# Layer 0 attention: transposes without padding, keys of the second batch earlier, and scores, all values, scores, other work in each group of heads

## The chip, the cores and the metric

The kernel runs on one core of a Trainium2 chip. A core has five engines with a queue each: TensorE (PE: matrix products, and transposes as products with an identity; its weight loads are listed apart as PEld), VectorE (DVE), ScalarE (ACT), GpSimd (POOL) and SyncE (SP, which here issues DMAs). Each works through its own instructions in order and waits on semaphores for the others. The metric is the device time of one execution in microseconds (us); lower is better.

## The reference

Four layers, each a cross attention and a feed-forward part with residuals and layer norms, on x of 4 batches x 256 tokens x 256, with a context of 512 tokens x 128 per batch. The change is in layer 0's attention:

```python
q = (x @ Wq + bq).reshape(b, s1, H, HD)          # H = 16 heads of HD = 16
k, v = from y_main @ Wk, y_main @ Wv             # 496 context tokens
k_dca, v_dca = from y_dca @ Wkv_dca              # the last 16 context tokens
q = _ln(q, qn_w, qn_b); k = _ln(k, kn_w, kn_b); k_dca = _ln(k_dca, kn_dca_w, kn_dca_b)
ctx = softmax(q k^T / 4) v + softmax(q k_dca^T / 4) v_dca      # per head
return ctx @ Wo + bo
```

The norms are per head, over its 16 values. The two softmaxes, over 496 and 16 tokens, are separate.

## The kernel before, in words

`bounded_path` (L837) computes everything in one launch; `general_path` runs only if a bound on the scores is exceeded. Layer 0 stands in a block with a manual schedule: on PE, ACT, DVE and POOL the order of the program is the order of the queue.

**Setup of batch 0** (L1482 to L1527): context transposes, layer norm, projections, `Scale` for queries and keys, `transposed`. `brow` shares the tile tag of kT, `rep` that of qT0; `norm_columns` (L1252) spreads the norm's weights from `rep` over the partitions as columns `cols`.

**Per batch.** `project_q` (L1170), `project_k` (L1186) and `project_v` (L1199) are products into PSUM; DVE adds the bias into `qk`, ACT copies values. `Scale` (L1212) normalises all heads: `square` on POOL (ACT in the setup), `sum` on DVE, `power` on ACT (Ln, then Exp), `product` on DVE, which writes the normalised heads into the single tile `pad`. There every head has 32 columns, of which the upper 16 are zero. `transposed` (L1306) turns pad's six chunks (two of queries, four of keys), with four transposes of 128x128 per chunk, one per group of heads, into one PSUM bank per chunk; the bank is evicted into qT or kT with the norm's weight and bias, by ACT for even chunks, by DVE for odd ones (L1330, L1328). In kT and qT a head then has a strip of 32 partitions, and 16 of them are used.

**Per group of four heads** (hg, four groups per batch). `scores` (L1334) for half the keys (kp 0 or 1): eight products (two chunks of keys x four heads), each head in its own strip of rows of the array; four PSUM banks, one per head; four exponentials on ACT (L1345) into pT. `values` (L1347): the four heads in four strips of columns, over two chunks of keys, plus four products for the 16 extra tokens (L1360). A column block of ones in the values gives the softmax sums. `quotient` (L1368): on DVE transpose, reciprocal, transpose, product (L1374 to L1382); on POOL the sums into oT. `output0` (L1389) projects a finished batch.

**Order.** One group runs behind: the values are those of the group before (`before`). The loop calls, per half i = 2 hg + kp: `scores`, `ahead(b, i)`, half the values, after the second half `quotient`, then `between(b, i)`. `ahead` and `between` (L1534, L1543) hold the other work, mostly the preparation of batch n = b + 1: i = 0 layer norm and context transposes, 1 queries, 2 keys and square, 3 values and sum, 4 power, 5 product and the statistics of batch n + 1, 6 the first three chunks of `transposed`, 7 the other three; `output0` of the batch before at 6 and 7. In the last batch the same places hold the first pieces of the feed-forward part (`Norm`, `Arrows`), the mask (`mf`, `pmk`, L1586 to L1591) and `output0`.

**PSUM.** Eight banks: two with tag "o" (the values' results), and a ring of six that scores, projections and transposes take in turn (L851). Whoever takes a bank waits until the one that had it six allocations before is evicted.

## Time and profile before

| what | value |
|---|---|
| median of 4 runs | 1416.97 us (1415.1 to 1422.18) |
| the profiled execution, its own time | 1416.62 us |
| its span | 1414.9 us |
| mean granted TensorE clock | 0.995 |
| first score matmul of layer 0 | 24.2 us |
| last value matmul ends, feed-forward products begin | 152.3 us |

Busy time of the engines in layer 0's stretches, in us, with the granted TensorE clock:

| stretch, us | holds | PE | DVE | ACT | POOL | clock |
|---|---|---|---|---|---|---|
| 24 to 56 | groups of batch 0 | 29.59 | 18.36 | 19.94 | 10.33 | 0.89 |
| 56 to 92.3 | batch 1 | 34.97 | 23.56 | 21.55 | 8.95 | 0.95 |
| 92.3 to 123.9 | batch 2 | 31.60 | 18.93 | 21.43 | 8.92 | 1.00 |
| 123.9 to 152.3 | batch 3 | 28.40 | 21.68 | 19.84 | 8.18 | 1.00 |
| 152.3 to 230 | feed-forward of layer 0 | 77.03 | 57.15 | 38.45 | 25.63 | 1.00 |

How to read it: in the timeline a line has the start, the busy time, the engine, the line of the code, the operation, out<-in, shapes and the number of instructions, and in brackets how long the engine was idle before and what ended that. "issue" means that it waited for nothing that the profile shows. Every fp32 product is two instructions, a transpose one. Matmul ends are modelled, so a busy PE is not PE at its peak; gaps between weight loads tell more.

### The profile page before, as it was taken

What the parts mean: (1) busy time and instruction counts of PE and PEld (TensorE: products, weight loads), DVE (VectorE), ACT (ScalarE), POOL (GpSimd) and SP (SyncE); (2) the same over time, 40 slices, a digit from 0 to 9 for tenths busy, and PEclk for the clock granted to TensorE, in tenths of its full rate; (3) what the DMA queues carried; (4) which work ended last, traced back from release to release, by engine and by line L of the source; (5) the groups of instructions that cost most, each with busy time, mean ns of one, the idle gap of its engine ahead of it and who ended that gap; (6) DMA issues with size and microseconds to landing.
All of it is one profiled execution on the core that took longest, in us unless ns stands there. A gap on an engine that the chain in (4) does not pass through costs nothing.

```text
span 1414.9 us, 20097 instructions
## 1 busy us (share of the span) xinstructions
PE 1395.2 (99%) x7339; PEld 921.7 (65%) x7339; DVE 893.9 (63%) x2004; ACT 586.3 (41%) x1156; POOL 677.4 (48%) x809
## 2 busy tenths in 40 slices
PE   9999999999999999999999999999999999999997
PEld 7566667566566666887555666666975656666666
DVE  5667874675765657654576656558655667566675
ACT  5567464433434332256443334333554343333331
POOL 3223322576554455132576654656214864445560
PEclk9999999999999999999999999999999999999999
DMA  5000120310000000273110000000421000000000
GB/s 164 2 1 2 60 75 16 77 37 1 8 0 8 1 8 1 65 219 95 38 53 8 16 1 8 0 0 16 145 71 60 5 1 1 1 1 0 1 1 33
DMA packets 48871, 46.01 MB, mean 33 GB/s; under 512 B 8185, under 2 KB 44762, under 8 KB 48764
## 3 DMA queue, kind: packets, MB, share of 16 engines
q1 hardware_dynamic: 45308, 36.90, 8.7%
q0 software_dynamic: 2352, 6.43, 1.6%
q8 instruction: 60, 0.98, 0.3%
q10 hardware_dynamic: 1104, 1.31, 0.3%
q14 instruction: 47, 0.39, 0.1%
HBM read 38.20 MB, written 6.42 MB: 32 GB/s over the span
## 4 chain that ended last, share of the span: by engine, by line
PE 91%; DVE 4%; POOL 2%; issue 1%; ACT 1%; DVEq 0%; POOLq 0%
PE ps L1856 22%; PE po L1864 22%; PE paq L1826 6%; PE pao L1826 5%; PE pbq L1826 4%; PE pbo L1826 4%; PE ps L1341 2%; PE paf L1425 2%; PE pgu L2379 2%; PE po L1351 2%; PE pyf L1475 2%; PE psh L2201 1%; PE py L1946 1%; PE pm L986 1%; PE pn L1002 1%
## 5 line engine op out<-in xcount | busy, mean ns | idle before, releaser
L1875 POOL TENSOR_TENSOR half<-pT 128x1024 f32<-128x1024 f32 x93 | 218.2, 2347 | 289.1 <-ACT pT L1859 217.3
L1856 PE MATMUL ps<-qT,cT 128*128 128x512 f32 x768 | 345.7, 593 | 0.0
L1864 PE MATMUL po<-pT,c_sb 128*128 128x512 f32 x768 | 345.3, 592 | 0.0
L1859 ACT ACTIVATE pT<-ps,mbias 128x512 f32<-128x512 f32 x384 | 263.8, 687 | 155.8 <-PE ps L1856 142.8
L1864 PEld LDWEIGHTS po<-pT,c_sb 128*128 128x128 f32 x768 | 146.0, 190 | 183.1 <-issue 183.1
L1856 PEld LDWEIGHTS ps<-qT,cT 128*128 128x128 f32 x768 | 139.0, 191 | 138.3 <-issue 136.7
L1868 ACT COPY oT<-po 128x512 f32<-128x512 f32 x96 | 56.3, 586 | 265.0 <-PE po L1864 265.0
L1911 POOL TENSOR_TENSOR oT<-oT,wide 128x512 f32<-128x512 f32 x90 | 114.3, 1290 | 17.3 <-DVE wide L1910 17.3
L1836 DVE TENSOR_TENSOR qT<-qT,paq 128x128 f32<-128x128 f32 x90 | 25.4, 282 | 95.1 <-ACT qT L1835 95.1
L1345 ACT ACTIVATE pT<-ps 128x512 f32<-128x512 f32 x128 | 65.9, 604 | 36.5 <-PE ps L1341 36.3
L1836 DVE TENSOR_TENSOR w<-w,pao 128x128 f32<-128x128 f32 x21 | 6.0, 285 | 106.6 <-ACT w L1835 106.6
L1883 DVE TENSOR_TENSOR half<-half 128x512 f32<-128x512 f32 x96 | 71.3, 742 | 2.7 <-POOL half L1873 2.5
L1885 DVE STREAM_TRANSPOSE turned<-half 128x512 f32<-128x512 f32 x96 | 68.3, 711 | 6.3
L1826 PE MATMUL paq<-xnT_a,m_sb 128*128 128x128 f32 x360 | 71.4, 280 | 0.0
L1826 PE MATMUL paq<-xx,m_x 128*128 128x128 f32 x360 | 69.6, 275 | 0.0
L1826 PEld LDWEIGHTS paq<-xnT_a,m_sb 128*128 128x128 f32 x360 | 57.3, 192 | 17.2 <-issue 8.7
L1889 DVE TENSOR_REDUCE sums<-turned 128x16 f32<-128x512 f32 x96 | 65.8, 686 | 3.3
L1826 PE MATMUL pao<-n_x,ox 128*128 128x128 f32 x336 | 65.2, 276 | 0.3 <-POOL ox L1752 0.3
L1835 ACT COPY qT<-paq 128x128 f32<-128x128 f32 x90 | 23.9, 265 | 94.1 <-PE paq L1826 94.1
L1910 DVE STREAM_TRANSPOSE wide<-rz 128x512 f32<-128x512 f32 x96 | 62.2, 685 | 0.1
L1839 DVE TENSOR_TENSOR qT<-qT,pbq 128x384 f32<-128x384 f32 x90 | 49.8, 554 | 9.4
L1826 PEld LDWEIGHTS paq<-xx,m_x 128*128 128x128 f32 x360 | 54.7, 192 | 0.0
(456 smaller groups left out, 2567.0 us busy)
## 6 DMA issues: line engine op xcount, KB each, us to landing
wq<-in_L_wqT SPq DMA_DIRECT2D x11, 512.0 KB, 5.3
wo<-in_L_wo SPq DMA_DIRECT2D x11, 512.0 KB, 7.0
yd<-yr SPq DMA_DIRECT2D x20, 128.0 KB, 4.7
w<-in_F_w SPq DMA_DIRECT2D x4, 512.0 KB, 3.3
xd<-xn_f SPq DMA_DIRECT2D x7, 256.0 KB, 2.1
wk<-in_L_wkT SPq DMA_DIRECT2D x11, 128.0 KB, 4.0
wv<-in_L_wvT SPq DMA_DIRECT2D x11, 128.0 KB, 5.0
x_sb<-in_x SPq DMA_DIRECT2D x4, 256.0 KB, 3.1
```

The source lines that it names most:

```text
L1345: nc.scalar.activation(pT[kp][:, j], ps[j], AF.Exp)
L1826: nc.tensor.matmul(p[:, at, :], lhsT=lhsT, rhs=rhs, start=(k == 0 and at == 0), stop=(k == len(of) - 1 and i == which[-1]),)
L1856: nc.tensor.matmul(ps, lhsT=cT[:, b, k * P : (k + 1) * P], rhs=qT, start=True, stop=True)
L1859: nc.scalar.activation(pT[:, k, :], ps, AF.Exp, bias=mbias[:, b, k : k + 1])
L1864: nc.tensor.matmul(po, lhsT=c_sb[:, b, k, :], rhs=pT[:, k], start=(k == 0), stop=(k == NK - 1))
L1868: done["head"] = nc.scalar.copy(raw, po).ins
L1875: nc.gpsimd.tensor_tensor(half, pT[:, 0:2], pT[:, 2:4], ALU.add)
L1883: nc.vector.tensor_tensor(part, half[:, 0], half[:, 1], ALU.add)
L1885: nc.vector.transpose(turned.rearrange("p f i -> p (f i)"), part)
L1889: nc.vector.tensor_reduce(sums[b, hp // 4][:, hp % 4, :], turned, AX.X, ALU.add)
L1910: nc.vector.transpose(wide, rzs[b, hp // 4][:, hp % 4, :, None].to_broadcast([P, NB, 32]))
L1911: eng.tensor_tensor(outs[b, hp], outs[b, hp], wide.rearrange("p f i -> p (f i)"), ALU.mult)
```

## The change

1. **Transposes without padding.** `pad` becomes [128, 6 chunks, 2, 128]: 16 heads of 16 columns without gaps, eight heads to a transpose. `transposed` is called for two chunks, with four transposes into one bank. A strip of 32 partitions now holds two heads (o = 0, 1). The keys are evicted as they are (kT uses two of its four planes); the queries are evicted twice, once per o, with columns `cols[:, o]` that are zero for the other head's 16 rows. Scores contract over 32 rows. ACT evicts queries o = 0 and keys 0 to 255, DVE queries o = 1 and keys 256 to 511, with a second small operation for the 16 extra tokens. Heads are numbered (q j o) instead of (q o j), so `wo0`, the biases and `wvo` are rearranged; `rep` has eight rows, filled by two POOL copies and one DVE copy; `brow` has its own tile.
2. **Early keys.** For batch n = 1: keys at i = 0 (before the layer norm's transposes), square at 1, sum at 2, power at 3, product at 4.
3. **Order per group.** Scores of half 0; all values of the group before, and its quotient; in group 3 all of `transposed(b + 1)`; scores of half 1; then `ahead` and `between` of both halves. In the first group of batch 0, which has no values, `between(0, 0)` stays between the two score calls.

```diff
-        brow = w0.tile([1, 2, 2 * D], F32, tag="kT", name="brow")
-        rep = w0.tile([1, 6, 4, 32], F32, tag="qT0", name="rep")
+        brow = l0.tile([1, 2, 2 * D], F32, tag="brow", name="brow")
+        rep = w0.tile([1, 8, 4, 2, HD0], F32, tag="qT0", name="rep")
...
-        pad = l0.tile([P, NQK * H0, 32], F32, tag="pad", name="pad")
-        nc.vector.memset(pad[:, :, HD0:], 0.0)
+        pad = l0.tile([P, NQK, 2, P], F32, tag="pad", name="pad")
...
-                self.dst = pad.rearrange("p (c h) x -> p c h x", h=H0)[:, a:z, :, :HD0]
+                self.dst = pad.rearrange("p c q (h x) -> p c (q h) x", x=HD0)[:, a:z]
...
-            for i in range(6):
+            for i in range(8):
...
-        def transposed(b, chunks):
+        def transposed(b, c0):
...
-            for c in chunks:
-                pt = bank("t", [P, 4, P], f"pT{b}_{c}")
-                for hg in range(4):
-                    r0 = c * H0 + 4 * hg
-                    nc.tensor.transpose(
-                        pt[:, hg, :], pad[:, r0 : r0 + 4, :].rearrange("p h x -> p (h x)"), ident
-                    )
...
+            pt = bank("t", [P, 2, 2, P], f"pT{b}_{c0}")
+            for c in range(2):
+                for q in range(2):
+                    nc.tensor.transpose(pt[:, c, q, :], pad[:, c0 + c, q, :], ident)
+            if c0 < NC:
+                src = pt.rearrange("p c q t -> p q c t")
+                for o in range(2):
+                    dst = qT.rearrange("p (q o) (c t) -> p o q c t", o=2, c=2)[:, o]
+                    if o:
+                        nc.vector.tensor_scalar(dst, src, cols[:, o, 0:1], cols[:, o, 1:2], ALU.mult, ALU.add)
+                    else:
+                        nc.scalar.activation(dst, src, AF.Identity, bias=cols[:, o, 1:2], scale=cols[:, o, 0:1])
+            else:
...
+                if k0:
+                    nc.vector.tensor_scalar(wide, src, cols[:, 2, 0:1], cols[:, 2, 1:2], ALU.mult, ALU.add)
+                    nc.vector.tensor_scalar(
+                        wide[:, :, 1, RD:], src[:, :, 1, RD:], cols[:, 3, 0:1], cols[:, 3, 1:2], ALU.mult, ALU.add
+                    )
                 else:
...
+                    nc.scalar.activation(wide, src, AF.Identity, bias=cols[:, 2, 1:2], scale=cols[:, 2, 0:1])
...
-                    r = slice(32 * j, 32 * j + HD0)
+                    r = slice(32 * j, 32 * j + 32)
                     k0 = (2 * kp + k) * P
                     nc.tensor.matmul(
-                        ps[j][:, k, :], lhsT=kTs[b][r, hg, k0 : k0 + P], rhs=qTs[b][r, hg, :], start=True, stop=True
+                        ps[j][:, k, :], lhsT=kTs[b][r, hg // 2, k0 : k0 + P], rhs=qTs[b][r, hg, :], start=True, stop=True
                     )
...
+        for o in range(2):
+            nc.gpsimd.tensor_copy(rep[:, 2 * o : 2 * o + 2, :, o, :], prm[:, 0, :, None, :].to_broadcast([1, 2, 4, HD0]))
...
             n = b + 1
             if n < B:
-                if i == 5:
+                if i == (4 if n == 1 else 5):
                     scale[n].product()
-                elif i == 7:
-                    transposed(n, range(3, NQK))
...
                 if i == 0:
+                    if n == 1:
+                        for k0 in range(0, NK, 2):
+                            project_k(n, k0)()
                     xnTs[n] = layernorm_T(xns[n], f"a0_{n}")
...
-                elif i == 2:
+                elif i == 2 and n > 1:
                     for k0 in range(0, NK, 2):
                         project_k(n, k0)()
+                elif i == 3 and n > 1:
+                    project_v(n)
+                if i == (1 if n == 1 else 2):
                     scale[n] = Scale(n, 0, NQK)
                     scale[n].square(False)
...
-                for kp in range(2):
-                    scores(b, hg, pT, kp)
-                    ahead(b, 2 * hg + kp)
-                    if before:
-                        if kp == 0:
-                            po = bank("o", [P, 2, S], f"po0_{b}_{hg}")
-                        values(*before, po, (2 * kp, 2 * kp + 1), kp == 1)
-                        if kp == 1:
-                            quotient(*before[:2], po, oTs[before[0]])
-                    between(b, 2 * hg + kp)
+                scores(b, hg, pT, 0)
+                if before:
+                    po = bank("o", [P, 2, S], f"po0_{b}_{hg}")
+                    values(*before, po, range(NK), True)
+                    quotient(*before[:2], po, oTs[before[0]])
+                else:
+                    between(b, 0)
+                if hg == 3 and b + 1 < B:
+                    for at in range(0, NQK, 2):
+                        transposed(b + 1, at)
+                scores(b, hg, pT, 1)
+                for i in (2 * hg, 2 * hg + 1) if before else (1,):
+                    ahead(b, i)
+                    between(b, i)
                 before = (b, hg, pT)
```

## The prediction

> **What bounds the kernel now.** I read the page first, then the chain of waits and the timeline of the first 230 us, then granted clock in half-microsecond stretches. The change touches only layer 0's attention, from its first score matmul at 24.2 us to the last value matmul at 152.3 us.

> ```profile
> span 1414.9 us, 20097 instructions
> ## 1 busy us (share of the span) xinstructions
> PE 1395.2 (99%) x7339; PEld 921.7 (65%) x7339; DVE 893.9 (63%) x2004; ACT 586.3 (41%) x1156; POOL 677.4 (48%) x809
> ```

> TensorE (PE) is the bound, so time saved on it counts until another engine makes it wait. The weight loads (PEld) in the timeline show what a turn costs when there is no other work between score calls (L1341) and value calls (L1351, L1360):

> ```profile
> 109.33 0.74 PEld L1341 LDWEIGHTS ps<-qT,kT 16*128 16x128 f32 x16 [0.33 <-issue]
> 110.41 0.59 PEld L1351 LDWEIGHTS po<-pT,vals 128*32 128x32 f32 x16 [0.33 <-issue]
> 111.41 1.01 PEld L1341 LDWEIGHTS ps<-qT,kT 16*128 16x128 f32 x16 [0.41 <-ACT pT L1345]
> 112.75 0.59 PEld L1351 LDWEIGHTS po<-pT,vals 128*32 128x32 f32 x16 [0.33 <-issue]
> 113.42 0.35 PEld L1360 LDWEIGHTS po<-pT,vals_d 128*32 128x32 f32 x8
> ```

> Each turn from scores to values leaves a gap of 0.33 us, each turn from values to anything 0.41; between L1351 and L1360, both values, there is none. I read the gap as the price of changing the array's shape. The other losses come from VectorE (DVE), as the chain of waits of 79 to 95 us shows:

> ```profile
> 79.05 1.76 DVE pad L1245
> 80.81 0.64 DVE z L1374
> ...
> 82.51 0.69 DVE o L1382
> 83.20 0.34 DVE st_a L918
> ...
> 84.31 0.58 DVE ve_a L920
> 84.90 0.72 DVE qT L1328
> 85.62 0.04 issue
> 85.67 1.13 PE ps L1341 x10
> ```

> Product, quotient, layer-norm statistics, then the eviction of one transposed bank: PE stood still from 84.34 to 85.67 because score bank j=3 is the ring bank that this eviction frees (six banks, taken in turn). The stop has a sequel in the granted clock. Columns: stretch, its length, PE's busy time (instructions), PEclk, DMA share, GB/s:

> ```profile
> 84.50:85.00 0.50, 0.00 (x0) 1.00 0.00 0
> 85.50:86.00 0.50, 0.33 (x6) 1.00 0.00 0
> 86.50:87.00 0.50, 0.50 (x4) 0.77 0.00 0
> 87.00:87.50 0.50, 0.50 (x4) 0.50 0.00 0
> 90.00:90.50 0.50, 0.50 (x16) 0.82 0.00 0
> ```

> From 86.8 to 90.2, 3.4 us, PE ran at half clock: up to 1.7 us lost for a wait of 1.33. The same follows the wait of 1.77 at 49.78 (half clock 52.7 to 56.1), and there is a third such stretch at 28.7.

> **What the change removes from PE.** (1) Transposes: 12 instead of 24 per batch. Twelve loads take 1.29 us (L1316 at 116.26), 0.107 each; 48 fewer are 5.1 us. (2) Turns. Value calls that are followed by something else: 29 before (15 groups of two halves, less the one that runs into the last call), 15 after: 14 x 0.41 = 5.7. Score calls: 32 such ends before, 27 after, since in five places (batch 0 after groups 1, 2, 3; batches 1 and 2 after group 2, counted from 0) nothing stands between two score calls: 5 x 0.33 = 1.7. Returns from full-size matmuls to scores (0.17 at 95.38): 21 to 15, 1.0; three returns from transposes to values at about 0.28 vanish, 0.8. Together 9.2. Sum: -14.3 us.

> **What it costs nothing, or little.** Scores now load 32 rows instead of 16: a 16-row load takes 185 ns, a 128-row one 190, and the matmuls 374 against 379, with four at once; 0 to +0.8 us, I take 0 (32 is nearer 16). The product writes pad densely; 1.76 for 1536 elements stays, as L1382's dense 512 take 0.69, no less per element. Evictions keep 512 elements at 0.79 (ACT) or 0.80 (DVE); ACT has 2 instead of 3 per batch, DVE 2 and a small one (0.33) instead of 4. POOL's two copies into rep (nearest POOL copy 0.3 each) run from 16.1, when POOL has nothing until 24.2, and end before norm_columns reads at 17.07; that has four more instructions at 0.12, 0 to 0.5, hidden since the key transposes wait for pad until 22.14 anyway: 0. The DMAs keep their number.

> **Waits that the new order makes.** Below, t is the start of a score call; its first exponential starts 1.23 later (109.33 to 110.56) and the four take 2.06.

> (a) Scores on scores: the ring has two free banks, the third and fourth come free when the first two exponentials of the call before end (t+1.8, t+2.3). PE wants them from t+0.94 on: 1.0 us. Once each in batches 1 and 2 and between batches 0 and 1: 3.0. In batch 0, `power` is queued on ACT ahead of the next group's exponentials and waits for the DVE sum; walking the queues on from the first scores at 23.7, the sum ends at 38.4, power at 39.05, and the exponentials that could start at 37.2 start then; PE stands at the ring three times, 1.0+1.2+1.3 = 3.5. In batch 3, 0.6. Sum 7.1.

> (b) Batches 1, 2, first group: xnT's copy now stands on ACT behind the second score call's exponentials: ready at 1.23+2.06+0.6 = t+3.9, while PE, after scores 1.07 and two sets of transposes 1.02, wants the query projection at t+2.1. 1.7 each: 3.4. Before, scores and values lay between.

> (c) Batches 1, 2: power stands behind the exponentials of the call at t: 3.29, Ln and Exp 0.6, product 2.63 (78.18 to 80.81): pad is ready at t+6.6; PE, after the next scores (done at t+2.75 with a), a turn of 0.33, all values 1.7 and a turn of 0.41, wants it at t+5.2. 1.4 each: 2.7.

> (d) Before the last score call of a batch: bank j=3 is the query transposes' bank. DVE must first do product, statistics 1.45 (not in batch 2), quotient 2.5, eviction 0.8. In batch 1: 6.6+1.45+2.5+0.8 = t+11.4; PE, after pad at 6.6, transposes 1.3 and three score matmuls, is there at t+8.4: 3.0. Batch 2: 9.9 against 8.4, 1.5. In batch 0 keys and product come one slot earlier; walked on from above, pad is ready at 44.0, the chain ends at 48.75, PE is there at 46.8: 1.9. Sum 6.4. Queued behind: four exponentials, both output projections, the next batch's scores.

> (e) Batch 3: pmk's transpose waits for mf, now behind the quotient on DVE (2.5, then the cast 0.64, PE has 1.1 to do): 2.1. (f) The last value call follows the last scores at once; its second half needs their exponentials (t+3.3; PE is there after 0.74+0.33 and half the values 0.67, at t+1.8, and its loads run on a little ahead): 1.3 to 1.5, I take 1.3.

> Added: 7.1+3.4+2.7+6.4+2.1+1.3 = 23.0. Removed: 1.77 and 1.33 (above), about 1.4 at 43.7 to 45, 1.2 in the start (keys need two evictions, not four), some 1.0 of small ones: 6.7. Waits: 23.0-6.7 = +16.3. Without the clock: -14.3+16.3 = +2.0.

> **Clock.** There are some seven places with waits over 1.3. Half clock costs nothing where PE would have waited anyway, as between (c) and (d), so I take five stretches at 1.5, 7.5, against 3 x 1.7 = 5.1 now: +2.4. Bounds: no more loss than now, 0; eight stretches at 1.7, +8.5. [...]

> Sum +4.4, against the profiled execution's 1416.62 (span 1414.9 plus 1.7 around it, 0.35 below the median of the runs shown): **1421 us**. After the attention PE is busy 77.03 of 77.70 us to 230, so what it gains or loses there is carried on.

> **Rivals.** *Clock gate (slower).* The waits of (b), (c), (d), (e) and (f) each draw a stretch of half clock: eight at 1.7 give +2.0+8.5 = +10.5, 1427. It decides from six to seven stretches on. For it: both waits of that size now did so. Against: a stretch that falls on a wait costs nothing. 0.28. *Turns aren't saved.* If the gaps were the tail of the matmuls and paid anyway, 9.2 come back: +13.6, 1430. Against: no gap at 113.42. 0.05. *Waits half as long (faster).* If exponentials and DVE keep up better than one chain after another, as where the query eviction precedes the quotient, 23.0 becomes 11.5: -14.3+11.5-6.7 = -9.5, 1407. Against: the queues are in program order, and the wait for j=3 is there now. 0.14. *My case*, 0.53.

> A measurement tells 0.5% (7.1 us) from no change. Within: 1409.9 to 1424.05. Range 1408 to 1431: the low end reaches to the faster case, the high one to both slower ones.

> **What would show it.** After: 48 transposes on L1316's successor; values in one run of 40 loads; PE waits of about 3 us for DVE qT before the last scores of batch 1, 1.7 for xnT before the query projections, 2 for mf; the attention ending near 156 instead of 152.3. PEclk in the slices 1 to 4 tells the clock. I am wrong if the j=3 wait is missing, or if PE runs through at full clock.

## The result, and the profile after

| | before | after |
|---|---|---|
| median | 1416.86 us (78 runs, 1413.07 to 1424.75) | 1419.81 us (48 runs, 1418.49 to 1423.09) |
| the profiled execution | 1416.62 us | 1421.25 us |
| first score load to last value load of layer 0's attention, by the timeline | 24.15 to 151.75: 127.6 us | 24.13 to 153.28: 129.15 us |
| stretches of half clock in it (3.4 us each) | 3 | 1 |

The ratio is 1.002, with a 95% interval of 1.0013 to 1.0026: 2.95 us slower, too little to count as a change by the bound of 0.5%, but not nothing. The page of the changed kernel begins:

```profile
span 1419.5 us, 19996 instructions
## 1 busy us (share of the span) xinstructions
PE 1390.4 (98%) x7295; PEld 918.8 (65%) x7295; DVE 889.5 (63%) x1999; ACT 584.1 (41%) x1152; POOL 678.4 (48%) x811
```

PE has less to do (1390.4 us instead of 1395.2) and needs longer: it waits more. The list of PE's waits between 20 and 160 us shows for what (us in total, times, longest):

```profile
PE pT L1319 <- DVE pad L1249: 3.6, 4, 1.2
PE pq L1178 <- ACT xnT_a L941: 3.3, 2, 1.7
PE pmk L1600 <- DVE mf L1596: 1.8, 1, 1.8
PE ps L1347 <- DVE qT L1325: 1.0, 1, 1.0
PE py L1399 <- DVE qT L1325: 1.0, 1, 1.0
PE ps L1347 <- ACT pT L1351: 0.9, 3, 0.3
PE ps L1347 <- ACT kT L1338: 0.4, 1, 0.4
PE ps L1347 <- DVE kT L1334: 0.4, 1, 0.4
```

The list of before in the same stretch:

```profile
PE pT L1316 <- DVE qT L1328: 1.8, 1, 1.8
PE ps L1341 <- DVE qT L1328: 1.3, 1, 1.3
PE pT L1316 <- ACT qT L1330: 0.5, 1, 0.5
PE pxn_a L938 <- DVE xn_a L926: 0.4, 1, 0.4
PE ps L1341 <- ACT pT L1345: 0.2, 1, 0.2
```

It comes to 4.2 us. In the changed kernel pad, xnT, mf and qT are there, as forecast. But PE's list counts modelled ends, and shows only 0.9 us for score calls that wait for exponentials. The weight loads show more. In the timeline of batch 1, group 2:

```profile
73.91 1.45 PEld L1357 LDWEIGHTS po<-pT,vals 128*32 128x32 f32 x32 [0.33 <-issue]
75.45 0.35 PEld L1366 LDWEIGHTS po<-pT,vals_d 128*32 128x32 f32 x8
76.21 1.16 PEld L1347 LDWEIGHTS ps<-qT,kT 32*128 32x128 f32 x20 [0.41 <-ACT pT L1351]
78.08 0.29 PEld L1347 LDWEIGHTS ps<-qT,kT 32*128 32x128 f32 x2 [0.71 <-ACT pT L1351]
78.57 0.72 PEld L1347 LDWEIGHTS ps<-qT,kT 32*128 32x128 f32 x10 [0.20 <-ACT pT L1351]
79.63 1.45 PEld L1357 LDWEIGHTS po<-pT,vals 128*32 128x32 f32 x32 [0.33 <-issue]
```

The values run in one piece, 73.91 to 76.21: 2.30 us. The two score calls behind them stand one on the other and take 3.42 us (76.21 to 79.63); a call with something else behind it takes 1.07 (89.36 to 90.43), two 2.14. The 0.71 and the 0.20 are the ring: the third and the fourth bank come free with the exponentials.

The chain of waits through the last group of batch 1, which answers to the one shown of before:

```profile
81.24 1.76 DVE pad L1249
83.00 0.35 DVE st_a L918
...
84.28 0.63 DVE z L1380
...
85.97 0.69 DVE o L1388
86.66 0.73 DVE qT L1325
87.39 0.04 issue
87.43 1.99 PE py L1399 x8
```

Product, statistics, quotient and eviction are still in a row on DVE. What waits for the eviction at the end is now the output projection (py), not the last score call.

The granted clock (columns as in the windows of before):

```profile
52.50:53.00 0.50, 0.50 (x8) 0.67 0.00 0
53.00:53.50 0.50, 0.50 (x6) 0.50 0.00 0
...
87.00:87.50 0.50, 0.07 (x1) 1.00 0.00 0
90.00:90.50 0.50, 0.50 (x16) 1.00 0.00 0
```

Half clock comes once in the attention, at 52.7; where before had it, at 86.8 to 90.2, the clock is full, though PE stood still just ahead of it (1.0 us for qT, up to 87.43).

**Where the time came from.** From the end of the attention to 560 us every product of the changed kernel starts 1.52 us later than in before's profile. Then, between 590 and 645 us, in layer 1's expert part, whose code is the same, it loses another 3.7 us; from there to the end the shift stays near 5.2. Experiments 8 and 11 come back to these 3.7 us.

### The profile page after: what moved, and what is told of

Read it like the earlier page. It is cut to its first block, busy times and chain, and to the rows that moved or that the text cites. A ratio compares the mean times of both kernels' runs of the same rounds, so it can differ in the third digit from the quotient of the medians.

```text
span 1419.5 us, 19996 instructions
## 1 busy us (share of the span) xinstructions
PE 1390.4 (98%) x7295; PEld 918.8 (65%) x7295; DVE 889.5 (63%) x1999; ACT 584.1 (41%) x1152; POOL 678.4 (48%) x811
## 4 chain that ended last, share of the span: by engine, by line
PE 89%; DVE 4%; POOL 2%; issue 2%; ACT 1%; DMA 1%; DVEq 0%; POOLq 0%; ACTq 0%
PE ps L1870 22%; PE po L1878 22%; PE paq L1840 6%; PE pao L1840 5%; PE pbq L1840 4%; PE pbo L1840 4%; PE ps L1347 2%; PE paf L1431 2%; PE pyf L1481 2%; PE po L1357 2%; PE psh L2215 1%; PE pgu L2393 1%; PE py L1960 1%; PE pm L986 1%; PE pn L1002 1%
## 5 line engine op out<-in xcount | busy, mean ns | idle before, releaser
L1351 ACT ACTIVATE pT<-ps 128x512 f32<-128x512 f32 x128 | 65.8, 605 | 35.3 <-PE ps L1347 35.3
```

The costliest lines, as they stand in the source:

```text
L1351: nc.scalar.activation(pT[kp][:, j], ps[j], AF.Exp)
```

## The experiments

Theory at the start: the order saves turns and gives them back as waits, made by the work that now stands behind the second score call. Rivals: half clock decides; the new transposes cost. "Attention" below is the time from the first score load to the last value load in a run's profile, with its stretches of half clock.

**1. The old order, the rest as changed.**

```diff
-                scores(b, hg, pT, 0)
-                if before:
...
-                    values(*before, po, range(NK), True)
+                for kp in range(2):
+                    scores(b, hg, pT, kp)
+                    ahead(b, 2 * hg + kp)
+                    if before:
...
+                        values(*before, po, (2 * kp, 2 * kp + 1), kp == 1)
...
+                    between(b, 2 * hg + kp)
```

In place 6 stands transposed(n, 0), in place 7 of `ahead` the other two.

> The changed kernel with the order of before: transposes without padding and early keys stay; scores, half the values, scores, the other half and the other work alternate as before, and the transposes stand in the places they had. Theory (the order saves turns but gives them back as waits, the unpadded transposes are a gain by themselves): the 48 transposes fewer give 48 x 0.107 = 5.1 us against before, two evictions fewer in the start about 1, so 1410 to 1412, ratio to before 0.996; 48 transposes in the trace, value loads in halves with a turn of 0.41 us after each, and the wait for the query bank before a batch's last score call still there. Rival 1 (the order is a gain, the new transposes and 32-row scores cost): slower than the changed kernel, 1421 or more. Rival 2 (half clock decides): three stretches of half clock in the attention as in before and a time within 2 us of before.

Measured: 1409.53 us, ratio 0.9939 (0.992 to 0.9959), half a microsecond under the range expected; attention 116.77 us, no half clock in it. The theory holds: the order alone costs 10.3 us against this kernel, and the other two parts gain 7.3. Its timeline shows the same kind of group as above:

```profile
70.61 1.01 PEld L1347 LDWEIGHTS ps<-qT,kT 32*128 32x128 f32 x16 [0.41 <-ACT pT L1351]
71.95 0.59 PEld L1357 LDWEIGHTS po<-pT,vals 128*32 128x32 f32 x16 [0.33 <-issue]
72.63 0.35 PEld L1366 LDWEIGHTS po<-pT,vals_d 128*32 128x32 f32 x8
73.39 0.74 PEld L1347 LDWEIGHTS ps<-qT,kT 32*128 32x128 f32 x16 [0.41 <-ACT pT L1351]
74.46 0.59 PEld L1357 LDWEIGHTS po<-pT,vals 128*32 128x32 f32 x16 [0.33 <-issue]
75.46 0.20 PEld L1319 LDWEIGHTS pT<-ident,pad 128*128 128x128 f32 x2 [0.41 <-ACT pT L1351]
```

Two score calls and two halves of values take 4.85 us (70.61 to 75.46); in the new order the same work takes 2.30+3.42 = 5.72. The halves take 1.44 and 1.00 with what follows them, 2.44 for the pair. One run takes 2.30. So joining two halves saves 0.14 us, not the 0.41 of a gap. The loads run ahead of the products (16 loads in 0.59, 32 in 1.45), and nearly all of the gap behind them is time that the products need anyway.

**2. The padded transposes in the new order.** The transposes, the score rows, `pad` and the numbering of heads are those of before; the loop and the early keys are the changed ones:

```diff
-                    for at in range(0, NQK, 2):
-                        transposed(b + 1, at)
+                    transposed(b + 1, range(NQK))
```

> The new order and the early keys with the padded transposes of before (24 transposes a batch, 16-row scores, heads as before; the bias row has a tile of its own, as in the changed kernel). Theory: 48 transposes more than the changed kernel, 5.1 us, and four evictions on DVE instead of two and a small one in front of the last score call of a batch; 1424 to 1428, ratio to before 1.005 to 1.008. Rival 1 (the 32-row scores or their evictions cost what the transposes save): within 1 us of the changed kernel, 1419 to 1421. Rival 2 (16-row scores draw half clock): more stretches of half clock than the two that the changed kernel's profile shows.

Measured: 1428.7 us, ratio 1.0073 (1.0047 to 1.0099); attention 132.69 us with three stretches of half clock. The transposes are a gain, 8.9 us in this order, but most of it is clock: the six runs here have a mean granted clock of 0.9925, those of the changed kernel 0.9969. One stretch (3.4 us at half clock, so 1.7 of some 1420) lowers this mean by 0.0012, so the difference is about 6 of the 8.9 us, and the second rival has its share. Of the 3.5 us by which the two profiled attentions differ, two stretches more of half clock make up about 3.2, at the price found in experiment 8, so the share of the 48 transposes isn't told apart here.

**3. Late keys in the new order.**

```diff
-                if i == (4 if n == 1 else 5):
+                if i == 5:
                     scale[n].product()
...
-                    if n == 1:
-                        for k0 in range(0, NK, 2):
-                            project_k(n, k0)()
...
-                elif i == 2 and n > 1:
+                elif i == 2:
```

Square, sum and power follow, one place later.

> The changed kernel without the early keys: batch 1 is prepared in the places that the other batches have (keys and square at 2, sum at 3, power at 4, product at 5). Theory: the early keys only move the start of one chain in batch 0; without them power no longer stands in front of the exponentials of batch 0 waiting for the sum, but pad comes one place later, so that the transposes for batch 1 wait about as long as they do for batches 2 and 3 (1.2 to 1.6 us instead of 0.9, and 1 us less in front of the first scores of batch 1): within 1.5 us of the changed kernel, 1418 to 1421. Rival (the early keys carry the change): 1423 or more.

Measured: 1423.99 us, ratio 1.0042 (1.0027 to 1.0057). The theory falls: the early keys are worth 4.2 us. About 3 of these are clock again (0.9948 against 0.9969). The timeline of batch 0 shows why:

```profile
47.84 1.76 DVE L1249 TENSOR_TENSOR pad<-qk,hr 128x1536 f32<-128x1536 f32 x1
...
49.71 1.34 PEld L1319 LDWEIGHTS pT<-ident,pad 128*128 128x128 f32 x12 [3.13 <-issue]
49.74 1.70 PE L1319 MATMUL pT<-ident,pad 128*128 128x128 f32 x12 [2.68 <-DVE pad L1249]
```

PE stands still for 2.68 us for pad, and 10.2 us of half clock follow (50.9 to 61.1).

**4. Four pieces of work moved back up.**

```diff
+                if hg == 0 and 0 < b < B - 1:
+                    xnTs[b + 1] = layernorm_T(xns[b + 1], f"a0_{b + 1}")
+                    context_T(b + 1)
+                    last_context(b + 1)
+                if hg == 2 and b + 1 < B:
+                    scale[b + 1].power()
                 scores(b, hg, pT, 1)
...
+        arrows[1] = Arrows(1)
+        arrows[1].vectors()
         po = bank("o", [P, 2, S], "po0_last")
```

The cast mf goes ahead of the quotient in the same way.

> The changed kernel with four pieces of work moved back up in the queues: the layer norm's and the context's transposes for batches 2 and 3 stand before the second score call of the first group instead of behind it; power stands before the second score call of group 2; the cast mf of batch 3 stands before that group's quotient; the first products of the feed-forward part's second piece stand between the last score call and the last values. Theory (the waits of the new order come from work queued behind the second score call): xnT 2 x 1.9, pad 2 x 1.6 less a turn of 0.4 each, mf 1.85 and 1.2 at the last values go, less two turns of 0.3: 3.8+2.4+1.85+1.2-0.6 = 8.6 us in the attention, which then ends near 145 instead of 153.8; 1410 to 1413, ratio to before 0.995 to 0.997. Rival 1 (the waits only move to the next consumer in the queues): the attention ends at 151 to 154, 1417 to 1420. Rival 2 (what the attention gains is lost in the expert part of layer 1, where the changed kernel's profile lost another 3.7 us between 590 and 645 us): the attention ends near 145 and the time stays above 1416.

Measured: 1414.86 us, ratio 0.9983 (0.9967 to 0.9999). Behind the attention the products start 5.3 us earlier than in the changed kernel, of 8.6 expected. The waits for xnT, mf and the last exponentials are gone from the list; pad still has 2.7 us in four places, and the score calls' loads, from the first of a call to its last, take 1.4 us more in all. So undoing (b), (c), (e) and (f) as far as it goes gives back 5.0 of the 10.3 us; the rest must be elsewhere.

**5. The transposes alone**: experiment 1 with the edit of experiment 3.

> Before with the transposes without padding alone: order of before, keys of batch 1 in their old place. It differs from e1_old_order only in the early keys. Theory A (the early keys matter only in the new order, where they shorten a chain that the order made late; in the order of before the queries' and keys' chain of batch 1 is ready in time either way): within 1.5 us of e1_old_order, 1408 to 1411. Rival B (the early keys are worth the 4.2 us that they are worth in the new order, in every order): 1412.5 to 1415, and a wait of some 2 us for pad in front of the transposes for batch 1.

Measured: 1413.72 us, ratio 0.9965 (0.9948 to 0.9981); attention 122.81 us with two stretches of half clock. The time is rival B's: the early keys gain 4.2 us here too. Its wait isn't there: PE waits 0.8 us for pad, as in experiment 1. What the early keys spare in this order is 1.4 us of waiting for xn ahead of batch 1's layer norm, where the key projections now stand, 1.4 us at the ring in a score call at 42.7 (loads in 2.12 us instead of 0.74), 0.5 us for qT, and some clock. One after another the three parts of the change are transposes -3.1, early keys -4.2, order +10.3; that they add up to the result, +3.0, is so by construction. Without the clock, at 1 - granted clock as the share of the span lost, they are about -3.6, -2.5 and +10.3.

**6. Filler.** Before, with 12 transposes more ahead of each of the two long waits:

```diff
-                for hg in range(4):
+                for hg in 4 * list(range(4)) if b in (1, 2) and c == 2 else range(4):
```

> Before with work added: for batches 1 and 2 the third chunk's four transposes are done four times over (12 more transposes each, 1.28 us, with the same result), just ahead of the two places where PE waits 1.77 and 1.33 us for a bank. Theory (those waits each draw a stretch of half clock of 3.4 us, which costs up to 1.7 us): the waits shrink to 0.5 and 0.1, the two stretches go, and the kernel gets faster by 2 to 3.4 us though it does more: ratio 0.9975 to 0.9985. Rival (half clock at these places falls on time that is lost anyway, or doesn't depend on the waits): 1417 to 1418.5, ratio 1.000 to 1.001.

Measured: 1414.11 us, ratio 0.9976 (0.9962 to 0.9991); attention 122.8 us, no half clock in it. More work, less time: 2.8 us. In before half clock followed waits of 1.77 and 1.33 us; with 0.5 and under 0.1 in their place this profile has none. A single profile doesn't tell, since experiment 8 has one stretch without any change. But over the 12 runs the granted clock is 0.9975, in before's 23 beside them 0.9959: about 2.3 of the 2.8 us.

**7. Statistics later.** Experiment 1 with DVE's statistics behind the query eviction:

```diff
-                if i == 5 and n + 1 < B:
-                    norms[n + 1] = Norm(n + 1, f"a0_{n + 1}")
                 if i == 6:
                     transposed(n, 0)
                     if n + 1 < B:
-                        xns[n + 1] = norms[n + 1].tokens()
+                        norms[n + 1] = Norm(n + 1, f"a0_{n + 1}")
+                if i == 7 and n + 1 < B:
+                    xns[n + 1] = norms[n + 1].tokens()
```

> e1_old_order with the layer-norm statistics of batch n + 1 moved on DVE from in front of the query eviction to behind it (from place 5 to 6, and what follows from 6 to 7). Theory (what is queued on DVE ahead of the eviction sets PE's wait for the bank): the waits of 1.84 and 1.83 us in front of the third transpose bank of batches 1 and 2 shrink by the 1.45 us of the statistics each: 2.5 to 3 us less than e1_old_order, 1406 to 1407.5, ratio to before 0.992 to 0.993. Rival (the statistics then delay the key evictions and the next layer norm, and the wait comes there): 1409 to 1411.

Measured: 1406.57 us, ratio 0.9917 (0.9894 to 0.994), 3.0 us under experiment 1: the theory holds. PE's wait for qT shrinks from 3.4 us (two times) to 0.3; pxn_a now waits 1.5 us for xn and pT 0.9 for y_sb, so that some of it moves, as the rival said.

**8 and 11. Both kernels again**, unchanged, for second profiles.

> The kernel before, unchanged, for a second profile. Question: the changed kernel's profile loses 3.7 us against before's between 590 and 645 us, in the expert part of layer 1, where the code is the same, and one stretch of half clock at 592 us. If that is a matter of the execution, this profile should have the expert part longer than the first one by 1 to 4 us, with the time in it; if the first profile is typical of before, the two agree there within 0.5 us. The first 150 us should agree within 2 us, half clock aside.

> The changed kernel, unchanged, for a second profile. If the 3.7 us between 590 and 645 us belong to the change, they are there again, within 0.5 us; if to the execution, as two profiles of before (1.3 us apart there) suggest, the expert part is 0 to 3 us longer than in before's first profile, and by another amount.

Measured: before 1417.37 us, attention 124.38 us with one stretch of half clock; the 127.6 with three differ by 3.2, so a stretch costs 1.6 us, and without any before's attention is about 122.8 (experiment 6, with its filler in the place of waits, has the same). After: 1421.1 us, attention 129.20, again with one stretch, so about 127.6 without. In the expert part the second profile of before is 1.3 us longer than the first, the second of after 2.1 longer than before's first, against 3.7. So it varies by the execution: over the other profiles it is 0.1 (experiment 7) to 4.5 us (experiment 10) longer. A stretch of half clock near the same product (589 to 591 us in the time of before's profile) is in 8 of the 14 profiles, among them that of experiment 6, which keeps the order of before. It goes with where the steps of 3.413 us lie (last section): in these 8 profiles one step of 3.413 us covers 3.04 us or more of a run of 32 small matmul instructions there (128x40, L2326, 4.06 us in the changed kernel), in the other 6 no step covers more than 2.84; in the first profiles it is 3.35 (after) and 2.23 (before). The rest of the 3.7 us is PE's wait for `xgT` (L2393): 2.1 us in both profiles of the changed kernel, but 0.2 in experiment 3, which has the new order too; what sets it stays open.

**9. Only the values joined.** The changed kernel, with the first half's other work back ahead of the second score call:

```diff
-                else:
-                    between(b, 0)
...
-                scores(b, hg, pT, 1)
-                for i in (2 * hg, 2 * hg + 1) if before else (1,):
-                    ahead(b, i)
-                    between(b, i)
+                for kp in range(2):
+                    if kp:
+                        scores(b, hg, pT, 1)
+                    ahead(b, 2 * hg + kp)
+                    between(b, 2 * hg + kp)
```

> The changed kernel with one thing of the order of before back: the other work of a group's first half stands ahead of the second score call again (scores, all values and quotient, in group 3 the transposes, work of the first half, scores, work of the second half). All values in one run and the transposes in one place stay. Theory (the loss is in the other work behind the second score call, not in the joined values): the xnT waits go (3.3 us of PE waiting), the waits for pad of batches 1 and 2 mostly (2.4), about 1 of the 1.8 for mf, and score calls behind score calls become fewer: 6 to 9 us less than the changed kernel, 1411 to 1414. Rival (joining the values and the transposes makes the loss, since ACT's exponentials no longer run beside half of the values): less than 3 us from the changed kernel, 1417 or more. Against e1_old_order's 1409.5, which has the halves apart, a saving of 0.41 us per joined pair, as forecast, would bring it to 1406 or below; a saving of 0.13 us (2.43 us for two halves in the trace, 2.30 for one run) can't.

**10. The same, with the statistics behind the evictions** (`Norm` in place 6, `tokens` in 7).

> e9_joined_values_only with the layer-norm statistics on DVE behind the query and key evictions, as in e7_statistics_later. Theory (as in e7, the statistics ahead of the query eviction make PE wait for the bank): the waits for DVE qT in front of the last scores of batch 0 and the output projection of batch 1 (1.0 us each in the changed kernel's list) go: 1.5 to 2.5 us less than e9. Rival: within 0.8 us of e9.

Measured: experiment 9 1420.05 us, ratio 1.0016 (0.9998 to 1.0033), attention 130.48 with three stretches; experiment 10 1416.1 us, ratio 0.9986 (0.9971 to 1.0001), attention 123.54 with none. My theory for 9 falls, the rival holds: xnT's waits are gone from the list, and the time is the changed kernel's. Some 2 us are gained and lost to the clock again (0.9955 in 12 runs, against 0.9969). Experiment 10 is 3.9 us under 9, more than the 1.5 to 2.5 expected; the waits for qT are gone, and about 2.5 of it is clock (0.9973). Experiments 10 and 7 differ by the joined values, the gathered transposes and what follows from both for DVE's queue, and neither has half clock in the attention: 123.54 against 115.89 us, 7.7 us. Summed over the profile of 10, the loads of the score calls, from the start of a call's first load to that of its last, take 31.2 us; in experiment 7 they take 20.7. Of the 10.5 us more, 3.8 lie in the call behind each batch's transposes and in the one after it, the rest in the other calls; smaller gaps elsewhere give some of it back. The larger part of the loss is thus the order on PE itself: a half of the values between any two score calls covers most of the exponentials' 2.06 us; one run covers one of two calls, and the other stands at the ring. The three banks of transposes in one place add to it. No run has the values joined and the transposes in their old places, so this split is read from one profile each.

**12. Statistics and tokens placed once more.** Experiment 7 with `Norm` behind `output0` in place 6, `tokens` in `ahead`, place 7, behind the transposes:

```diff
                     transposed(n, 2)
                     transposed(n, 4)
+                    if n + 1 < B:
+                        xns[n + 1] = norms[n + 1].tokens()
```

> e7_statistics_later with the statistics also behind the output projection's eviction, and the normalised tokens of batch n + 1 ahead of the last quotient instead of behind it. Theory: the waits that e7 still shows for y_sb (0.9 us) and xn (1.5 us in three places) go: 1 to 2 us less than e7, 1404.5 to 1405.5, ratio to before 0.991 to 0.992. Rival (the quotient, now later, holds the last value bank or the output projection up): within 0.5 us of e7 or slower.

Measured: 1404.64 us, ratio 0.9908 (0.9885 to 0.993), the best here, 12.5 us under before and 1.9 under experiment 7, as the theory expected; attention 113.07 us. The list of PE's waits from 23 to 158 us is then, in full:

```profile
PE pT L1319 <- DVE pad L1249: 0.8, 1, 0.8
PE ps L1347 <- ACT kT L1338: 0.4, 1, 0.4
PE pT L1319 <- DVE qT L1325: 0.3, 1, 0.3
```

## Why the prediction was right as a sum, and where it was wrong

Forecast +4.4 us, measured +2.95. "Without the clock" the forecast had +2.0, half clock +2.4. The granted clock, averaged over 69 runs of before and 50 of after, is 0.9958 and 0.9969: 1.5 us gained by the clock, so +4.4 without it. The sum is right in part by luck: errors of both signs cancel in it, and the profiled execution's 1421.25 us meets the 1421 only with the 3.7 us of the expert part. Of the signs named, the 48 transposes, the values in runs of 40 loads, and the waits for xnT (1.7) and mf (1.8) came. The 3 us for qT ahead of batch 1's last scores did not, which the prediction called a sign of being wrong; 1.0 us for it came ahead of the output projection. The attention ended at 153.8 us, not near 156. The prediction says that its range reaches down to the faster case; its low end, 1408, stops just short of that case's 1407. Step by step:

- **Transposes, -5.1.** In the attention 36 of the 48 count, 3.8 us at 0.107. The other 12 are batch 0's; the first scores start at 24.13 instead of 24.16 (and with the clock granted later 24.92, experiment 3, against 24.93, experiment 8), so neither they nor the 1.2 us of waits that I took off the start, 2.5 us together, gained anything.
- **Early keys, no price given.** Wrong: 4.2 us in either order, the clock's share included. The chain of batch 0 was worked out only with them, never without, so that what the keys add to it or spare it couldn't show.
- **Turns, -9.2: the step that failed.** Its largest term, 14 exits from value calls at 0.41 = 5.7, took each gap for the price of a change of shape. Here is one run of the changed kernel with its products:

```profile
90.43 1.45 PEld L1357 LDWEIGHTS po<-pT,vals 128*32 128x32 f32 x32 [0.33 <-issue]
90.43 1.93 PE L1357 MATMUL po<-pT,vals 128*32 128x256 f32 x32
...
91.97 0.34 PEld L1366 LDWEIGHTS po<-pT,vals_d 128*32 128x32 f32 x8
92.18 0.61 PE L1366 MATMUL po<-pT,vals_d 128*32 128x256 f32 x8
92.73 0.74 PEld L1347 LDWEIGHTS ps<-qT,kT 32*128 32x128 f32 x16 [0.41 <-issue]
```

  The loads end ahead of the products, and the next loads begin when these are nearly through. 15 pairs at 0.14 saved 2.1 us. This is the premise of the rival "turns aren't saved", for the values; that there is no gap where two value lines meet doesn't speak against it. Whether the change of shape holds the next loads up isn't told apart here; the products need nearly all of the time either way. The smaller terms (0.33 behind scores, 0.17 ahead of them) are still in the trace as gaps.
- **Waits added, 23.0.** Right in the sum; over the loads I count about 22.4: each score call's loads beyond the undisturbed 0.56 us, each other gap beyond its turn. (a) 7.1 forecast, 8.8 found (1.6 instead of 1.0 where score calls meet); (b) 3.4 and 3.3; (c) 2.7 and 2.9; (d) 6.4 and 4.3; (e) 2.1 and 1.8; (f) 1.3 and 1.3. In (d) the last score call of a batch waits for the key eviction on ACT (0.4 to 0.5 us); the ring gave the query bank to what comes later, the next batch's scores in batch 0, the output projection in batch 1, nothing in batch 2.
- **Waits removed, 6.7.** Too little. The attention without half clock is 127.6 - 122.8 = +4.8 us; with -3.8, -2.1, some -3.5 for the smaller turns and +22.4 this leaves 8.2 us, against 5.5 without the start's. I had left out the small stops of before's score calls. This one is a remainder, and its parts were not measured.
- **Clock, +2.4.** Wrong in sign: five stretches forecast, one came. Waits as long as those that cost a stretch in before passed without one in after (3.3 us for xnT in two waits, up to 60.7 and to 96.6). The price was right, 1.6 for 1.5; the number can't be had from the length of a wait.

So four errors of 2.5 to 4 us each, the values' turns and the start on one side, the clock and the waits removed on the other, nearly cancel, and that is luck; the mechanism, turns and transposes given back as waits in the queues, holds. Its largest term was (a). The work behind the second score call, which I took as the theory of the experiments, gave back 5.0 of the 10.3 us when moved up (experiment 4).

## What to carry to other kernels

A gap behind a run of loads can be the tail of the products that they ran ahead of (here gaps of 0.41 us, of which joining two halves saved 0.14): compare the whole time of the two forms, first load to next other load, before counting gaps as saved. Where one engine's pieces cover another's (here half of the values the exponentials of a score call), joining the pieces removes the cover from every second one (the score calls' loads took 31.2 us in experiment 10, 20.7 in experiment 7, though the transposes, too, stand in other places there). Price each part of a change by itself, the small one too: here the two parts without the new order were worth 7.3 us, and the order hid them.
